# Attention block with two-level Strassen products: some VectorE work of the first image placed elsewhere, and inner sums of two outer factors taken in one instruction

## The chip, the cores and the metric

The kernel runs on one core of one Trainium2 chip. The metric is the device time of one execution in microseconds (us); lower is better. In the profile the engines are called PE (TensorE, matrix products), PEld (its weight loads), DVE (VectorE), ACT (ScalarE), POOL (GpSimd) and SP (SyncE, which issues DMAs).

## The reference

Sixteen images x of 512 channels by 32x32 places, all in fp32. Each is normalised over 8 groups of 64 channels, goes through attention with 4 heads of 128 channels over its 1024 places, is projected, and is added to x.

```python
xg = x.reshape(b, NUM_GROUPS, -1)
xn = ((xg - mu) * rsqrt(var + EPS)).reshape(b, c, h, w) * gamma + beta
q, k, v = split(einsum('oc,bchw->bohw', qkv_w, xn) + qkv_b, 3)   # to heads
attn = softmax(einsum('bhnd,bhmd->bhnm', q, k) * dh ** -0.5)
out = einsum('bhnm,bhmd->bhnd', attn, v)
return x + einsum('oc,bchw->bohw', proj_w, out) + proj_b
```

## The kernel before

**Products.** Scores and the weighted sum over values are plain fp32 products of 128 x 128 by 512 columns (`scores`, L964, tile `s`; `weighted_sum`, L1058, tile `po`). The three linear layers go by Winograd's form of Strassen's scheme, which takes seven products for eight, applied twice: seven outer factors, and in each seven inner products. The right-hand operand is called b. In one level, its four blocks b11, b12, b21, b22 give four sums: t1 = b12 - b11, t2 = b22 - t1, t3 = t2 - b11, t4 = b21 - t2; t2 needs t1, and t3 and t4 need t2. `FACTORS` says which operands each of the products 1 to 7 takes: product 1 b11, product 2 b21, product 3 b22, product 4 t4, product 5 t1, product 6 t2, product 7 t3.

**Outer level.** `halves` (L324) makes the outer blocks of an image out of four tiles of 128 x 1024 (x, the normalised input, or o, the output of the heads): each tile holds two blocks of 512 columns side by side. The outer t1 is written over b12, in the same tile; t2, t3 and t4 have tiles of 128 x 512 of their own, two of each (`KC` is 2). `sums_of_b` (L342) computes them on VectorE.

**Inner level.** `two_levels` runs the outer factors in four groups, `OUTER` = (1, 5), (2, 6), (7, 4), (3): a group holds one or two outer factors, whose inner products stand side by side in one PSUM bank of 512 columns, 256 columns for each factor. So group 0 works on the outer b11 and t1, group 2 on the outer t3 and t4. `make_sum` (L657) computes the inner sums of a group: one tile of 128 x 512 takes the sum for both outer factors, and a loop over i issues one VectorE subtraction of 128 x 256 for each. `mm` (L690) issues the products, ACT copies partial results out of PSUM (L565), VectorE adds them up (L715), adds groups together (L768) and adds the bias (`finish`, L827 for queries and keys, L943 and L946 for the projection). A group's products run in the order 1, 2, 6, 5, 7, 4, 3 (`ORDER`).

**Which sums are made where.** Each image has two query/key calls (`qk_groups`, pairs 0 and 1), one value call (`v_groups`) and one projection call (`proj_groups`). The calls of pair 0 make the inner sums and, from the second image on, keep them in DRAM, from where the value call loads them; pair 1 and the projection make their own. For pair 0 of the next image, the sums t1 and t2 of group 0 are taken with high priority behind the last running sum of the softmax denominators in the stage of head 1 (`added[b - 1, 1, NB - 1]`, L983).

**Order.** Each engine's instruction order is fixed before the run by a planner. It takes instructions in the order of their priorities, as they become ready by its own estimate of durations. The kernel steers it: `high_priority` moves an instruction ahead, `issue_after` puts one behind another on its engine, `keep_in_program_order` (called `pin` in the first image) holds the written order.

**First image.** `open_image` (L1328) writes the order out by hand. After the statistics of the upper two channel chunks, the value products of the first image start (`v_units`, one level, L845, with weights `wv`); the lower two chunks go through their group statistics, whose reciprocal root is taken by POOL (L89, `rstd`). Meanwhile VectorE computes sums of the value weights: s1 = a21 + a22, s2 = s1 - a11, s3 = a11 - a21 (written over a21), s4 = a12 - s2. Then `shift` yields, for each lower chunk, the shift (L1351), and the chunk's first half is normalised (L111 on VectorE for chunk 2, L108 on ACT for chunk 3), then the second halves. The outer t2 follows (L1342), then t3 (L1421), s3 of the value weights (L1422), t4 (L1424) and s4 (L1425), which are not pinned but stand behind t2.

Of the kernel before, what the change touches and what calls it, by code (L numbers as in the profile page):

```python
# [10 lines left out]
F32 = mybir.dt.float32  # L11
# [5 lines left out]
P = 128  # L17
# [4 lines left out]
HALF = 512  # L22
# [156 lines left out]
KC = 2  # L179
Q = 256  # L180

OUTER = ((1, 5), (2, 6), (7, 4), (3,))
# [3 lines left out]
def fast_path(ctx, tc, x, sources, out, consts, flag, dims):  # L186
# [6 lines left out]
    nc = tc.nc  # L193
    B, C, N, NCC, NH2, NB, GC, SCALE = dims
# [9 lines left out]
    tpool = ctx.enter_context(tc.tile_pool(name="t", bufs=1))  # L204
# [113 lines left out]
    def normalise(b, c, half, on_scalar=True):  # L318
        t = xs[b, c][:, ts(half, HALF)]
        sc, sh, i = scaled[b, c]  # L320
        return norm.apply(t, t, sc, sh, i, on_scalar)


    def halves(tiles, prefix):  # L324

        b = {
            f"b{r + 1}{h + 1}": [tiles[2 * r + k][:, ts(h, HALF)] for k in range(KC)]
            for r in range(2) for h in range(2)
        }
        b["t1"] = b["b12"]  # L330
        for n in ("t2", "t3", "t4"):
            b[n] = [
                tpool.tile([P, HALF], F32, tag=f"{prefix}{n}{k}", name=f"{prefix}{n}{k}")
                for k in range(KC)
            ]
        return b

    def sums_of_b(b, rows=(1, 2, 3), chunks=range(KC)):
# [149 lines left out]
    wv, beside, between = {}, {}, {}  # L488
# [58 lines left out]
    def run(units):  # L547
        for u in units:
            u()
# [54 lines left out]
    def two_levels(name, site, b, blocks, finish, sums="make", homes="BBBB", prepare=None):  # L604
# [7 lines left out]
        haves, pairs = [{} for _ in OUTER], {}  # L612
# [10 lines left out]
        def sum_tile(g, m):  # L623
            k = int(m[1]) - 1
            tag = f"in_{m}" if homes[g] == "B" else f"ot{2 + k // 2}{k % 2}"
            if homes[g] == "C":
                if k % 2 == 0:
                    pairs[g] = ppool.tile([P, N], F32, tag="p", name=f"{name}_{g}_{m}")
                t = pairs[g][:, ts(k % 2, HALF)]
            else:  # L630
                t = tpool.tile([P, HALF], F32, tag=tag, name=f"{name}_{g}_{m}")
            haves[g][m] = t.rearrange("p (i q) -> p i q", q=Q)
            return haves[g][m][:, : len(OUTER[g])]

        def inner_block(g, i, m):
            if m[0] == "t":
                return haves[g][m][:, i, :]
            outer = blocks()[FACTORS[OUTER[g][i]][1]]
            return outer[int(m[1]) - 1][:, ts(int(m[2]) - 1, Q)]

        def make_sum(g, m):
            n = len(OUTER[g])
            to = sum_tile(g, m)
            a, c = {
                "t1": ("b12", "b11"), "t2": ("b22", "t1"), "t3": ("t2", "b11"),
                "t4": ("b21", "t2"),
            }[m]
            with ExitStack() as order:
                if sums == "keep" and g == 0 and m in ("t1", "t2"):


                    order.enter_context(tc.issue_after(added[b - 1, 1, NB - 1].ins))
                    order.enter_context(tc.high_priority(URGENT))
                if (b, site) == (0, 1) and (g > 0 or m in ("t3", "t4")):
                    order.enter_context(tc.issue_after(beside["scores"].ins))
                for i in range(n):
                    nc.vector.tensor_sub(  # L657
                        to[:, i, :], inner_block(g, i, a), inner_block(g, i, c)
                    )
            if sums == "keep":  # L660
                t = dpool.tile([P, n, Q], F32, tag=f"{m}_{g}", bufs=1, name=f"kept_{m}_{g}")
                inner_kept[b, g, m] = t
                nc.gpsimd.dma_start(t, to)  # L663
# [292 lines left out]
    def where(s):  # L956
        bh, j = divmod(s, NB)
        return (*divmod(bh, HEADS), j)
# [362 lines left out]
    def warm(n, name):  # L1321

        acc = ps_s.tile([P, HALF], F32, tag="s", name=name)
        for _ in range(n):
            ins = nc.tensor.matmul(acc[:, :P], avg, avg, start=True, stop=True)  # L1325
            tc.keep_in_program_order(ins)

    def open_image(units):  # L1328


        pin = tc.keep_in_program_order
        mvs[0] = gn.tile([P, NCC, 2], F32, tag="mv", name="mv_0")
        upper, lower = slice(0, KC), slice(KC, NCC)

        def steps(these, *pinned):
            for i, step in enumerate(these):
                ins = step()
                if i in pinned:
                    pin(ins)

        def sum_(o, i, j, add=False):
            return pin((nc.vector.tensor_add if add else nc.vector.tensor_sub)(o, i, j))  # L1342

        def shift(r):

            mu, sc = norm.result
            sh = gn.tile([P, KC], F32, tag="sh", name="sh")
            for i, c in enumerate(range(r.start, r.stop)):
                o = slice(i, i + 1)
                scaled[0, c] = sc, sh, i  # L1350
                pin(nc.vector.scalar_tensor_tensor(  # L1351
                    sh[:, o], mu[:, o], sc[:, o], beta_sb[:, c : c + 1], ALU.mult, ALU.add
                ))
                yield c

        def stats_on_scalar(c):
            mean, var = mvs[0][:, c, 0:1], mvs[0][:, c, 1:2]
            junk = lpool.tile([P, N], F32, tag="tt", name="junk_0")
            off = gn.tile([P, 1], F32, tag="off", name="off")
            root = math.sqrt(N)  # L1360
            pin(nc.scalar.activation(
                junk, xs[0, c], AF.Identity, scale=1.0 / N, accum_out=mean
            ))
            pin(nc.scalar.mul(off, mean, -1.0 / root))
            pin(nc.scalar.activation(
                junk, xs[0, c], AF.Square, bias=off, scale=1.0 / root, accum_out=var
            ))

        warm(14, "warm_0")
        for c in range(KC):  # L1370
            steps(norm.chunk_steps(mvs[0], xs[0, c], c), 0, 1, 2)
        with tc.high_priority(URGENT):
            g = norm.group_steps(mvs[0][:, upper, :], 0, -1.0)
            steps(g[:1], 0)
            warm(2, "warm_1")
            steps(g[1:7], 0, 1, 2, 3, 4, 5)
            warm(9, "warm_2")

        stats_on_scalar(KC)
        pooled = g[7]()  # L1380
        pin(pooled)
        with tc.issue_after(pooled.ins):
            for t, src in ((qkb_sb, qk_b), (vb_sb, v_b), (projb_sb, proj_b)):
                nc.gpsimd.dma_start(t, src)
        steps(g[8:], 0)
        for c in shift(upper):
            pin(normalise(0, c, 0, False))
        for c in range(KC):
            pin(normalise(0, c, 1))
        steps(norm.chunk_steps(mvs[0], xs[0, NCC - 1], NCC - 1), 0, 1, 2)  # L1390
        xb[0] = halves([xs[0, c] for c in range(NCC)], "x")
        bl = xb[0]
        g = norm.group_steps(mvs[0][:, lower, :], KC, -1.0)

        def urgent(these, *pinned):
            with tc.high_priority(URGENT):
                steps(these, *pinned)

        between[1, 1, 0] = [lambda: urgent(g[:1], 0)]
        run(units[:2])  # L1400
        sum_(bl["t1"][0], bl["b12"][0], bl["b11"][0])
        sum_(wv["s1"], wv["a21"], wv["a22"], True)
        urgent(g[1:5], 0, 1, 2, 3)
        sum_(bl["t1"][1], bl["b12"][1], bl["b11"][1])
        between[0, 5, 0] = [lambda: urgent(g[5:6], 0)]
        run(units[2:3])
        urgent(g[6:7], 0)
        with tc.high_priority(URGENT):
            beside["pow"] = g[7]()
            pin(beside["pow"])  # L1410
        sum_(wv["s2"], wv["s1"], wv["a11"])
        urgent(g[8:], 0)
        for c in shift(lower):
            pin(normalise(0, c, 0, c % 2 == 1))
        for c in range(KC, NCC):
            pin(normalise(0, c, 1, c % 2 == 1))
        for k in range(KC):
            last = sum_(bl["t2"][k], bl["b22"][k], bl["t1"][k])
        with tc.issue_after(last.ins):
            for k in range(KC):  # L1420
                nc.vector.tensor_sub(bl["t3"][k], bl["t2"][k], bl["b11"][k])  # L1421
            nc.vector.tensor_sub(wv["s3"], wv["a11"], wv["a21"])  # L1422
            for k in range(KC):
                nc.vector.tensor_sub(bl["t4"][k], bl["b21"][k], bl["t2"][k])  # L1424
            nc.vector.tensor_sub(wv["s4"], wv["a12"], wv["s2"])  # L1425
        return last
# [19 lines left out]
    for s in range(steps + 1):  # L1446
        units = []
        if s < steps:
            b, h, j = where(s)
# [9 lines left out]
        for half in range(NH2):  # L1459
# [21 lines left out]
            n = (len(units) + 1) // 2  # L1481
# [150 lines left out]
```

## Time and profile before

| what | us |
|---|---|
| median of 3 runs | 3137.39 (3136.8 to 3137.7) |
| the profiled execution | 3137.81 |
| its span, first to last instruction | 3136.2 |
| PE busy (10412 matmul records, two for each fp32 product) | 3129.6 |
| VectorE busy (4683 instructions) | 2667.9 |
| ACT busy | 1447.4 |
| POOL busy | 512.2 |
| mean granted TensorE clock | 1.000 |

By stage (windows of the trace, us):

| stage | length | PE busy | DVE busy | ACT busy |
|---|---|---|---|---|
| value products of the first image, 11.14 to 35.7 | 24.56 | 24.56 | 23.09 | 7.26 |
| first query/key products, 35.7 to 62.2 | 26.50 | 26.25 | 26.19 | 9.62 |
| all images after that, 62.2 to 3111 | 3048.80 | 3048.80 | 2596.09 | 1422.00 |

How to read the profile: a row of a timeline gives start, duration, engine, line, operation, "out<-in" by the program's tile names with buffer numbers left out, the shape, and how many instructions of that kind were merged into the row; in square brackets stands the engine's idle time before it and what ended it. A row of the groups gives the busy time, the mean duration in ns of one, and the idle time before. Durations of instructions on one engine can overlap: the next VectorE instruction may start before the one before it ends. Ends of matmuls are modelled, so PE's real losses are read from the distances of starts. One image takes about 194.5 us; the same pattern returns at that distance.

### The profile page before, as it was taken

The numbers are of one execution on the slowest core, as the hardware profiler recorded it, in microseconds if no ns is written. First come the engines' busy times: TensorE is split into PE (matmuls) and PEld (weight loads), VectorE is DVE, ScalarE is ACT, GpSimd is POOL, SyncE is SP. The second block draws the span as 40 slices with busy tenths as digits, with TensorE's granted clock in tenths as the row PEclk, the third lists the DMA queues.
The fourth block names the chain that finished last, engine by engine and source line by source line (L and its number), as shares of the span: only waits on it lengthen the run. The fifth ranks groups of instructions, "written<-read, shape, count | busy, mean of one in ns | idle before, by whom it ended". The sixth has DMA issues, their size and how long they took to land.

```text
span 3136.2 us, 34085 instructions
## 1 busy us (share of the span) xinstructions
PE 3129.6 (100%) x10412; PEld 2200.4 (70%) x10412; DVE 2667.9 (85%) x4683; ACT 1447.4 (46%) x2655; POOL 512.2 (16%) x922
## 2 busy tenths in 40 slices
PE   9999999999999999999999999999999999999999
PEld 7567777777777777777777777777777777777765
DVE  8988889788897888978799787997879978799787
ACT  3545435354354543545435454454534535345433
POOL 0121121111211112111121101212012120121200
PEclk9999999999999999999999999999999999999999
DMA  5554554545555455554555545555455554555641
GB/s 176 170 192 149 197 172 165 165 153 189 175 167 165 147 194 172 166 168 145 197 170 167 170 144 191 169 176 168 145 185 172 176 175 140 179 169 178 193 128 45
DMA packets 210363, 522.59 MB, mean 167 GB/s; under 512 B 32368, under 2 KB 65776, under 8 KB 210176
## 3 DMA queue, kind: packets, MB, share of 16 engines
q1 hardware_dynamic: 132320, 278.26, 29.1%
q0 software_dynamic: 65184, 207.75, 19.6%
q10 hardware_dynamic: 12672, 34.35, 3.3%
q8 instruction: 86, 1.41, 0.2%
q14 instruction: 101, 0.83, 0.1%
HBM read 387.07 MB, written 133.17 MB: 166 GB/s over the span
## 4 chain that ended last, share of the span: by engine, by line
PE 100%; DVE 0%; issue 0%
PE po L1058 28%; PE s L964 28%; PE qk_x L690 12%; PE qk_y L690 9%; PE pp_x L690 6%; PE v_x L690 6%; PE pp_y L690 4%; PE v_y L690 4%; PE v_x L845 0%; PE warm L1325 0%; PE lx L1163 0%; PE v_y L845 0%; PE last_x L690 0%; PE v_z L845 0%; PE lv L1163 0%; PE lw L1163 0%
## 5 line engine op out<-in xcount | busy, mean ns | idle before, releaser
L964 PE MATMUL s<-qk,qk 128*128 128x512 f32 x2048 | 1045.8, 592 | 0.2 <-DVE qk L827 0.2
L1058 PE MATMUL po<-p,v 128*128 128x512 f32 x2048 | 1045.4, 592 | 0.0
L970 ACT ACTIVATE p<-s 128x512 f32<-128x512 f32 x1024 | 610.5, 596 | 877.6 <-PE s L964 853.3
L1058 PEld LDWEIGHTS po<-p,v 128*128 128x128 f32 x2048 | 616.2, 301 | 375.2 <-issue 258.5
L983 DVE TENSOR_TENSOR tot<-tot,p 128x1024 f32<-128x1024 f32 x385 | 470.0, 1221 | 133.6 <-ACT p L970 132.6
L964 PEld LDWEIGHTS s<-qk,qk 128*128 128x128 f32 x2048 | 389.0, 190 | 68.9 <-issue 12.9
L690 PEld LDWEIGHTS qk_x<-qk_t,w 128*128 128x128 f32 x1344 | 254.4, 190 | 153.3 <-issue 95.5
L690 PE MATMUL qk_x<-qk_t,w 128*128 128x256 f32 x1344 | 353.3, 379 | 0.0
L565 ACT COPY qk_u<-qk_x 128x512 f32<-128x512 f32 (+1 forms) x256 | 136.3, 532 | 238.0 <-PE qk_x L690 238.0
L896 POOL DMA_DIRECT2D vd<-vu x120 | 66.4, 553 | 957.3 <-DVE vu L888 955.1
L715 DVE TENSOR_TENSOR qk_r<-qk_y,qk_u 128x512 f32<-128x512 f32 (+1 forms) x256 | 158.2, 618 | 34.2 <-ACT qk_u L565 21.7
L947 POOL DMA_DIRECT2D out_y<-y x120 | 65.1, 543 | 643.4 <-DVE groups L300 401.3
L715 DVE TENSOR_TENSOR v_r<-v_y,v_u 128x512 f32<-128x512 f32 (+1 forms) x120 | 76.1, 634 | 107.6 <-ACT v_u L565 77.4
L690 PE MATMUL v_x<-v_t,w_v 128*128 128x256 f32 x630 | 165.3, 379 | 0.0
L690 PE MATMUL pp_x<-pp_t,w_proj 128*128 128x256 f32 x630 | 165.3, 379 | 0.0
L663 POOL DMA_DIRECT2D kept_t<-qk_t x240 | 129.6, 542 | 217.0 <-DVE qk_t L657 191.3
L690 PEld LDWEIGHTS pp_x<-pp_t,w_proj 128*128 128x128 f32 x630 | 119.7, 190 | 62.5 <-issue 35.9
L690 PEld LDWEIGHTS v_x<-v_t,w_v 128*128 128x128 f32 x630 | 119.7, 190 | 59.0 <-issue 34.4
L901 POOL DMA_DIRECT2D v<-vd x240 | 139.9, 590 | 68.7 <-issue 38.2
L690 PE MATMUL qk_y<-x,w 128*128 128x256 f32 x512 | 142.0, 379 | 0.0
L827 DVE SCALAR_TENSOR_TENSOR qk<-qk_r,qkb_sb,qk_r 128x512 f32<-128x512 f32 x192 | 137.7, 746 | 1.7
L888 DVE STREAM_TRANSPOSE vu<-vt 128x512 f32<-128x512 f32 x120 | 135.6, 1130 | 0.7 <-DMA vd<-vu 0.7
(251 smaller groups left out, 4417.6 us busy)
## 6 DMA issues: line engine op xcount, KB each, us to landing
w<-kept SPq DMA_DIRECT2D x90, 512.0 KB, 3.9
kept_t<-qk_t POOLq DMA_DIRECT2D x180, 256.0 KB, 2.8
v_t<-kept_t SPq DMA_DIRECT2D x180, 256.0 KB, 2.8
w<-kept SPq DMA_DIRECT2D x90, 384.0 KB, 3.4
rinv<-row ACTq DMA_DIRECT2D x63, 512.0 KB, 4.9
x<-in_x POOLq DMA_DIRECT2D x60, 512.0 KB, 4.8
vd<-vu POOLq DMA_DIRECT2D x120, 256.0 KB, 2.9
v<-vd POOLq DMA_DIRECT2D x240, 128.0 KB, 4.1
```

Source lines behind the costliest of these rows:

```text
L565: nc.scalar.copy(t[n][:, :width], t["x"][:, :width])
L663: nc.gpsimd.dma_start(t, to)
L690: latest["product"] = nc.tensor.matmul(acc[:, ts(i, Q)], have["w"][t][:, i, slot, :], inner(i, bn), start=(first and i == 0), stop=True, s ...
L715: latest["outer"] = nc.vector.tensor_add(dst, view(a), view(c))
L827: return nc.vector.scalar_tensor_tensor(st[b, h][:, ts(half, HALF)], a, qkb_sb[:, i : i + 1], c, ALU.add, ALU.add)
L888: nc.vector.transpose(u.rearrange("p (q i j) -> p j q i", q=n, i=BLK), t.rearrange("p (j q i) -> p j q i", q=n, i=BLK),)
L896: nc.gpsimd.dma_start(rows[which][ts(h, P), :], u)
L901: nc.gpsimd.dma_start(vs[b, pair][ts(q, BLK), half].rearrange("m h (k i) j -> m (h k) (i j)", k=n), rows[which].rearrange("(k m) (q e) -> ...
L964: latest["score"] = nc.tensor.matmul(sc, ks[b, h][:, ts(j, P)], qs[b, h][:, ts(half, HALF)], start=True, stop=True)
L970: exps[s] = nc.scalar.activation(ps[s][:, ts(half, HALF)], sc, AF.Exp, scale=SCALE)
L983: added[b, h, j] = nc.vector.tensor_add(tot[b, h][:, i], tot[b, h][:, i], ps[s][:, i])
L1058: summed = nc.tensor.matmul(po[half], v_block(b, h, j), ps[s][:, i], start=(j == 0), stop=(j == NB - 1),)
```

## The change

There are three edits.

1. `halves` puts the outer t3 and t4 of x side by side into one tile of 128 x 1024 (for o they stay apart), and keeps the two-block tiles under the keys 0 (b11 and t1, for x and o) and 2 (t3 and t4, for x). `make_sum` then takes, for groups 0 and 2 of the query/key calls and group 0 of the projection, both outer factors in one subtraction of 128 x 512 whose operands are two pieces of 256 columns each (`both_blocks`); the other groups keep the loop. The last image's projection, which has no such tiles, keeps the loop too.
2. In `open_image`, s3 of the value weights is computed directly behind s2, pinned, instead of between the outer t3 and t4.
3. In `open_image`, `list(shift(lower))` issues the shifts of both lower chunks first and then the normalisations, instead of shift, normalisation, shift, normalisation.

```diff
@@ halves @@
+        b[0] = tiles[:KC]
+        b["t2"] = tiles_of("t2")
+        if prefix == "x":
+            b[2] = tiles_of("t34", N)
+            b["t3"], b["t4"] = ([t[:, ts(i, HALF)] for t in b[2]] for i in range(2))
+        else:
+            b["t3"], b["t4"] = tiles_of("t3"), tiles_of("t4")
@@ two_levels @@
+        def both_blocks(g, m):
+            if m[0] == "t":
+                return haves[g][m][:, : len(OUTER[g]), :]
+            t = blocks()[g][int(m[1]) - 1].rearrange("p (i c q) -> p i c q", i=2, c=2)
+            return t[:, :, int(m[2]) - 1, :]
...
-                for i in range(n):
-                    nc.vector.tensor_sub(
-                        to[:, i, :], inner_block(g, i, a), inner_block(g, i, c)
-                    )
+                if g in blocks():
+                    nc.vector.tensor_sub(to, both_blocks(g, a), both_blocks(g, c))
+                else:
+                    for i in range(n):
+                        nc.vector.tensor_sub(
+                            to[:, i, :], inner_block(g, i, a), inner_block(g, i, c)
+                        )
@@ open_image @@
         sum_(wv["s2"], wv["s1"], wv["a11"])
+        sum_(wv["s3"], wv["a11"], wv["a21"])
         urgent(g[8:], 0)
-        for c in shift(lower):
+        for c in list(shift(lower)):
             pin(normalise(0, c, 0, c % 2 == 1))
...
         with tc.issue_after(last.ins):
             for k in range(KC):
                 nc.vector.tensor_sub(bl["t3"][k], bl["t2"][k], bl["b11"][k])
-            nc.vector.tensor_sub(wv["s3"], wv["a11"], wv["a21"])
             for k in range(KC):
                 nc.vector.tensor_sub(bl["t4"][k], bl["b21"][k], bl["t2"][k])
```

More of the change, by code (lines that the diff above doesn't have):

```diff
@@ L330, in halves, with tiles_of @@
         b["t1"] = b["b12"]
-        for n in ("t2", "t3", "t4"):
-            b[n] = [
-                tpool.tile([P, HALF], F32, tag=f"{prefix}{n}{k}", name=f"{prefix}{n}{k}")
+        def tiles_of(n, width=HALF):
+            return [
+                tpool.tile([P, width], F32, tag=f"{prefix}{n}{k}", name=f"{prefix}{n}{k}")
                 for k in range(KC)
             ]
+        b[0] = tiles[:KC]
[5 more added lines that the diff above has]
+            b["t3"], b["t4"] = tiles_of("t3"), tiles_of("t4")
         return b
```

## The prediction

> **What bounds the kernel.** I read the page first: busy shares (part 1), then the chain that ended last (part 4).
>
> ```profile
> PE 3129.6 (100%) x10412; PEld 2200.4 (70%) x10412; DVE 2667.9 (85%) x4683; ACT 1447.4 (46%) x2655; POOL 512.2 (16%) x922
> ...
> PE 100%; DVE 0%; issue 0%
> ```
>
> TensorE (PE) is the bound from end to end. Of the span of 3136.2 us, 6.6 are visibly idle on PE: 1.7 before its first matmul and about 4.5 behind its last, where no edit reaches. What PE loses besides is hidden in records that begin a little late, so I compared the starts of its matmuls with the usual spacing (0.430 us for 512 columns, 0.216 for 256). Beyond that spacing PE loses 4.4 us in all: 1.3 before 35 us, 1.7 between 35 and 62 us, 0.07 once in each of images 2 to 15 (0.94 together), 0.4 at the tail. All that this change can win lies in the second and third of these.
>
> Then the timeline of VectorE (DVE) in the first image, where two waits stand:
>
> ```profile
> 15.81 0.69 DVE L1342 TENSOR_TENSOR wv<-wv 128x512 f32<-128x512 f32 x1
> 17.12 0.16 DVE L76 TENSOR_TENSOR sc<-rstd,gamma_sb 128x2 f32<-128x2 f32 x1 [0.62 <-POOL rstd L89]
> ...
> 18.73 0.69 DVE L1342 TENSOR_TENSOR xt<-x,x 128x512 f32<-128x512 f32 x1
> 19.83 0.69 DVE L1342 TENSOR_TENSOR xt<-x,x 128x512 f32<-128x512 f32 x1 [0.40 <-ACT x L108]
> ```
>
> Last, the place in the steady images where an inner sum is closest to holding PE. I went through the spare time of every product behind the DVE row that feeds it; this one is the shortest of all sums, and it looks the same in images 2 to 15 (image 2 shown: DVE, weight loads, PE).
>
> ```profile
> 331.46 0.76 DVE L657 TENSOR_TENSOR qk_t<-x 128x256 f32<-128x256 f32 x2
> 332.14 0.76 DVE L657 TENSOR_TENSOR qk_t<-x,qk_t 128x256 f32<-128x256 f32 x2
> 332.67 0.79 PEld L690 LDWEIGHTS qk_x<-qk_t,w 128*128 128x128 f32 x4 [0.38 <-issue]
> 332.81 0.69 DVE L946 TENSOR_TENSOR y<-y,pp_r 128x512 f32<-128x512 f32 x1
> 332.84 1.03 PE L690 MATMUL qk_x<-qk_t,w 128*128 128x256 f32 x4
> 333.41 0.75 DVE L943 SCALAR_TENSOR_TENSOR y<-pp_r,projb_sb,y 128x512 f32<-128x512 f32 x1
> 333.70 1.03 PE L690 MATMUL qk_y<-qk_t,w 128*128 128x256 f32 x4
> ```
>
> The first row is t1 of outer factors 1 and 5, the second their t2; product 6 (qk_x at 332.84) reads t2, product 5 (qk_y at 333.70) reads t1. t2 of the first factor is done at 332.14 + 0.42 = 332.56.
>
> **The change, part by part.** *s3 moved.* One 128x512 subtraction (start to start 0.60) leaves its place at 21.64 and goes behind s2 into the 0.62 idle before 17.12: 15.81 + 0.60 = 16.41, next free 17.01. It fits, so it costs nothing; if rstd came sooner it would cost at most 0.60 on the normalisation. No other reader of the raw a21 is left by then (s1 read it at 13.71). It issues no DMA; SP's stores of wv_a can go some 4 us earlier, with the weight loads already issued before them. *Both shifts first.* The second shift moves from 18.03 to about 17.5, so ACT's normalise of chunk 3 starts about 0.45 before its 18.28, and the 0.40 wait at 19.83 goes. The first normalise on DVE is later by about 0.1; it was done at 18.12, and the weight load that needs it stands at 18.44.
>
> *Two sums in one.* Eight pairs fewer in each of 32 query/key calls (groups 0 and 2) and four in each of 15 projections (group 0): 256 + 60 = 316 pairs. A pair takes 0.67 (331.46 to 332.14 is 0.68), one 512-wide instruction 0.60 (332.81 to 333.41), so 0.07 each, 22 us of DVE time. The strided views cost nothing by the nearest rows:
>
> ```profile
> L657 DVE TENSOR_TENSOR qk_t<-x,qk_t 128x256 f32<-128x256 f32 x256 | 105.9, 433 | 2.2 <-PE qk_x L690 0.7
> L456 DVE TENSOR_TENSOR w<-w,w 128x256 f32<-128x256 f32 x6 | 2.6, 428 | 0.0
> ```
>
> L456 reads and writes two pieces of 128 apart from each other, L657 one piece. Almost all of the 22 us is off the path: DVE idles again between 289 and 306 us waiting for PE and ACT, so what is saved before that is waited away. In the first image DVE is hardly idle from 20.4 to 56 us and gains 0.60 + 0.40 + 8 x 0.07 = 1.6 us, but PE's 1.7 us lost there end mostly with ACT's copies of qk_x and with the chain last product, eviction, L827, first score. DVE ends 0.12 of it alone (at 44.87) and some 0.2 of the end chain: I take 0.3 gained, bounds 0 and 1.2 (all stalls that DVE ends). The 0.07 per image is an eviction at 327.09, behind DVE rows that are not merged and run without idle from 305: I take 0, bound 0.94.
>
> **What the merge takes away.** t2 reads what t1 writes. Now t1 of the second factor lies between, and hides the latency. Merged, t2 stands directly behind its own input. Rows for that:
>
> ```profile
> 315.07 0.42 DVE L657 TENSOR_TENSOR pp_t<-o 128x256 f32<-128x256 f32 x1
> 315.40 0.15 DVE L101 TENSOR_TENSOR sh<-beta_sb,t 128x4 f32<-128x4 f32 x1
> 315.48 0.74 DVE L943 SCALAR_TENSOR_TENSOR y<-pp_r,projb_sb,y 128x512 f32<-128x512 f32 x1
> 316.14 0.68 DVE L715 TENSOR_TENSOR pp_r<-pp_y,pp_u 128x512 f32<-128x512 f32 x1
> 316.74 0.41 DVE L657 TENSOR_TENSOR pp_t<-o,pp_t 128x256 f32<-128x256 f32 x1
> ...
> 320.68 0.68 DVE L715 TENSOR_TENSOR pp_r<-pp_y,pp_u 128x512 f32<-128x512 f32 x1
> 321.40 1.22 DVE L768 TENSOR_TENSOR pp_r<-pp_r,pp_r 128x1024 f32<-128x1024 f32 x1
> ```
>
> At 321.40 a dependent instruction starts 0.72 behind its input instead of 0.60. At 315.07 a single t1 and its t2 stand 1.67 apart: the planner, which fixes each engine's order beforehand, put three others between. And a late release costs PE this much: the eviction done at 327.09 held a product due at 327.18 (its pair takes 0.66 instead of 0.59), so the loss is release + 0.16 - due. Product 6 is due at 332.84, hence t2 has to be done by 332.68. The three ways:
>
> - A, t2 directly behind: 331.46 + 0.72 + 0.69 = 332.87, loss 0.19 an image, 14 images: 2.7 us.
> - B, one 512-wide between (L946 is ready): 331.46 + 0.60 + 0.60 + 0.69 = 333.35, loss 0.67, 14 times 9.4; image 1 (due 138.30, t1 at 136.31) about 0.1 more: 9.5 us.
> - C, as B on DVE, but PE's order changes too: product 5 needs only t1 (done by 332.15) and lasts 0.86; with it first, product 6 is due at 333.70, past 333.35 + 0.16, loss 0.
>
> Behind the waiting t2 stand L946 and L943 of the projection's outputs, which go to DMA; no product waits for them. The other merged sums have over 1 us to spare (t3 of the same group, next, 1.07).
>
> The Trainium skill, "VectorE: DVE Perf Modes", section "The DRAIN you can't avoid", says that a next op waits for the pipe whether chained or not, and that a semaphore between two costs nothing extra. By that, t2 would follow 0.60 behind t1 and A would cost 0.07 x 14 = 1.0 us instead of 2.7; the row's 0.72 differs from it, and I go by the row. The same page's section "Rules for kernel authors" asks for fewer ops and not fewer semaphores, and speaks for the merge; it says nothing of a dependent one.
>
> **Which way.** I take C as likeliest. The planner picks by readiness: in the first image's second call PE took qk_y<-qk_t at 64.79 before qk_x<-qk_t at 66.51, against the written order. With t2 0.8 us later than now, product 5 should be taken first. Sum: 3137.81 of the profiled run (span 3136.2 and 1.6 around it) - 0.3 = 3137.5; the median shown lies 0.4 lower, at 3137.39, so **3137.1**.
>
> **Rivals.** B is the slower one. It decides when t2 is done past 332.68 while the planner still thinks it ready for product 6. For it: the planner is off by some tenths here already, since it had PE wait at 327.18 in 14 images, and an eviction (L715 at 329.40) is taken 1.5 us after the product it reads (at 327.18, 0.66 long) is done. Against it: it needs an error of at least some 0.5 us in this direction. Time: 3137.4 - 0.3 + 9.5 = 3146.6. A: 3137.4 - 0.3 + 2.7 = 3139.8; against it that the planner fills such gaps whenever something is ready. A further rival is that all DVE-ended stalls go (1.2 + 0.9): 3135.3; even that is 0.07%, so nothing here can be faster by over 0.2% (6.3 us), about what a measurement of this kernel can tell from no change. Last, that other orders change with so many durations and PE is held in new places, bounded only by B's size: 0.05.
>
> **Chances.** C 0.44, A 0.15, full gain 0.05, B 0.31, other slower 0.05. Same = 0.44 + 0.15 + 0.05 less 0.01 for an unseen gain = 0.63; slower 0.36; faster 0.01. The likeliest's own range is 3136.0 to 3138.0; it leaves out more than 2 in 10, so the range reaches to B and its error: 3135.8 to 3147.5.
>
> **What would show it.** DVE: 4683 - 316 = 4367 instructions on the page, L657's successors 512 wide at about 690 ns, no 0.62 and 0.40 waits before 20 us. PE at about 332.8: qk_y<-qk_t before qk_x<-qk_t (C), the old order with the weight load 0.25 late (A) or 0.7 late (B), "PEld qk_x <- DVE qk_t" new in the waits. Wrong if PE loses time at other products, or if the 35 to 62 us stretch gets longer.

## The result, and the profile after

The changed kernel takes 3148.67 us (median of 7 runs, 3148.44 to 3149.54); the kernel before, run beside it on the same chip, 3137.35 (7 runs, 3136.8 to 3137.7). The ratio is 1.0036, 95% interval 1.0027 to 1.0046: 11.3 us slower. In the profiled executions the span grew from 3136.2 to 3147.2, by 11.0 us (the profiled execution of the kernel before, 3137.81, lies 0.5 above its median), and the rest of this section looks for those 11.0. Images are counted from 0.

The page of the changed kernel: busy shares (part 1), the chain that ended last (part 4), and from the groups the row of the linear layers' products.

```profile
PE 3133.0 (100%) x10412; PEld 2199.2 (70%) x10412; DVE 2650.6 (84%) x4367; ACT 1447.9 (46%) x2655; POOL 511.9 (16%) x922
...
PE 85%; DVE 12%; issue 2%; ACT 0%; DMA 0%; DVEq 0%; POOL 0%
...
L710 PE MATMUL qk_x<-qk_t,w 128*128 128x256 f32 x1344 | 354.6, 380 | 7.5 <-DVE qk_t L674 7.5
```

VectorE has 316 instructions fewer and 17.3 us less busy time, and the kernel is slower. The chain, PE alone before, now runs over VectorE for 12% of the span; that isn't time lost, only the way back from the places where a product waited for a sum. The last row names them: 7.5 us of visible idle time ahead of products that read `qk_t`, ended by `make_sum` (now L674). The waits of PE count them (engine, tile and line, what it waited for: us in total, times, the longest):

```profile
PE qk_x L710 <- DVE qk_t L674: 7.5, 15, 0.5
PE warm L1345 <- DVE avg L247: 1.7, 1, 1.7
PE pm L82 <- DVE mv L52: 0.5, 1, 0.5
PE s L984 <- DVE qk L847: 0.2, 1, 0.2
```

Fifteen times: once in each image from the second on. The timeline of image 2 at the place that the prediction showed:

```profile
332.21 0.68 DVE L674 TENSOR_TENSOR qk_t<-x 128x512 f32<-128x512 f32 x1
...
332.71 1.02 PE L1078 MATMUL po<-p,v 128*128 128x512 f32 x2
332.81 0.68 DVE L966 TENSOR_TENSOR y<-y,pp_r 128x512 f32<-128x512 f32 x1
333.41 0.68 DVE L674 TENSOR_TENSOR qk_t<-x,qk_t 128x512 f32<-128x512 f32 x1
334.01 0.74 DVE L963 SCALAR_TENSOR_TENSOR y<-pp_r,projb_sb,y 128x512 f32<-128x512 f32 x1
334.20 0.73 PEld L710 LDWEIGHTS qk_x<-qk_t,w 128*128 128x128 f32 x4 [1.18 <-ACT p L990]
334.24 1.10 PE L710 MATMUL qk_x<-qk_t,w 128*128 128x256 f32 x4 [0.50 <-DVE qk_t L674]
...
335.17 1.03 PE L710 MATMUL qk_y<-qk_t,w 128*128 128x256 f32 x4
```

t1 of both outer factors, one projection row (L966), t2 of both. The two records of `po` keep PE until 332.71 + 2 x 0.43 = 333.57; there product 6 was due. t2 is done at 333.41 + 0.68 = 334.09, the weight load begins at 334.20 and the product at 334.24: 0.67 us lost (0.50 of it shows as idle, because the ends of matmuls are modelled). Its four records take 1.10 instead of 1.03, another 0.07. PE keeps the old order, product 6 (qk_x<-qk_t) before product 5 (qk_y<-qk_t). In images 2 to 15 the loss is 0.74 each time; in image 1, where a 128x1024 transpose (L1012, 1.23 us) stands between t1 and t2, it is 0.66. 14 x 0.74 + 0.66 = **11.0 us**, as much as the spans differ. Smaller terms beside it cancel: the first value product starts 0.12 later, the trace ends 0.34 sooner behind its last product, and in image 6 a `qk_y` product loses 0.24, the only new loss of PE at another product. Its weight load waits there for a VectorE row, 15 us after VectorE itself has waited 0.80 for a DMA:

```profile
1223.14 0.73 PEld L710 LDWEIGHTS qk_y<-x,w 128*128 128x128 f32 x4 [0.38 <-DVE qk_r L735]
1223.15 1.13 PE L710 MATMUL qk_y<-x,w 128*128 128x256 f32 x4
```

The same pair, a DMA wait of 0.8 to 0.9 us and then a loss at `qk_y`, stands in experiments 7 and 8 and in no other kernel here (experiment 4 has a DMA wait of 0.41 at that place and no loss); whether the change brings the DMA wait about wasn't tried.

The first image, VectorE, where the two waits stood:

```profile
15.93 0.69 DVE L1362 TENSOR_TENSOR wv<-wv 128x512 f32<-128x512 f32 x1
16.54 0.68 DVE L1362 TENSOR_TENSOR wv_a<-wv,wv_a 128x512 f32<-128x512 f32 x1
17.24 0.16 DVE L76 TENSOR_TENSOR sc<-rstd,gamma_sb 128x2 f32<-128x2 f32 x1
...
18.73 1.33 DVE L1362 TENSOR_TENSOR xt<-x,x 128x512 f32<-128x512 f32 x2
```

Both waits are gone: s3 fills the first (16.54), and the two `xt` rows now stand back to back. VectorE's work in the stage of the first query/key products (35.7 to 62.2 us before, 35.8 to 62.3 now) fell from 26.19 to 24.75 us. PE's loss there, by the starts of its matmuls, went only from 1.69 to 1.65: the 0.12 at 44.87 went, and 0.08 came at 46.12.

### The profile page after: what moved, and what is told of

It is laid out like the page before. It is cut to its first block, busy times and chain, and to the rows that moved or that the text cites. A ratio compares the mean times of both kernels' runs of the same rounds, so it can differ in the third digit from the quotient of the medians.

```text
span 3147.2 us, 33761 instructions
## 1 busy us (share of the span) xinstructions
PE 3133.0 (100%) x10412; PEld 2199.2 (70%) x10412; DVE 2650.6 (84%) x4367; ACT 1447.9 (46%) x2655; POOL 511.9 (16%) x922
## 4 chain that ended last, share of the span: by engine, by line
PE 85%; DVE 12%; issue 2%; ACT 0%; DMA 0%; DVEq 0%; POOL 0%
PE s L984 24%; PE po L1078 23%; PE qk_x L710 12%; PE qk_y L710 9%; PE v_x L710 6%; PE v_y L710 4%; PE pp_x L710 3%; DVE tot L1003 2%; PE pp_y L710 2%; DVE y L966 2%; DVE pp_r L735 1%; DVE y L963 1%; DVE pp_r L788 1%; DVE pp_t L677 1%; DVE qk_t L674 1%
## 5 line engine op out<-in xcount | busy, mean ns | idle before, releaser
L1003 DVE TENSOR_TENSOR tot<-tot,p 128x1024 f32<-128x1024 f32 x385 | 469.4, 1219 | 129.1 <-ACT p L990 128.9
```

What stands on the lines that cost most here:

```text
L1003: added[b, h, j] = nc.vector.tensor_add(tot[b, h][:, i], tot[b, h][:, i], ps[s][:, i])
```

## The experiments

Eight kernels were run. Theory: the whole loss is product 6 of group 0 in the kept calls, held because t2 ends later, and nothing else in the change matters to the time.

**1. The first image's edits alone** (the kernel before with edits 2 and 3).

```diff
+        sum_(wv["s3"], wv["a11"], wv["a21"])
...
-        for c in shift(lower):
+        for c in list(shift(lower)):
...
-            nc.vector.tensor_sub(wv["s3"], wv["a11"], wv["a21"])
```

> The kernel before with the two edits of the first image alone (s3 behind s2, both shifts first), no merged sums. Theory (all of the loss sits at product 6 of group 0 in the calls that keep their sums, and comes from the merged t1 and t2): within 0.3 us of the kernel before, so 3137.0 to 3137.5; PE's 1.7 us lost between 35 and 62 us shrink by 0.1 at most. Rival (the moved work of the first image holds PE later): 3138 or more, with new losses before 62 us.

Measured: 3137.19 us against 3137.23, ratio 1.0000 (0.9990 to 1.0009). PE loses 1.65 us between 35 and 62 us, as in the changed kernel. The edits of the first image neither cost nor bring anything that can be measured.

**2. The changed kernel, with the kept t1 and t2 of group 0 in their loop again.**

```diff
+                early = sums == "keep" and g == 0 and m in ("t1", "t2")
-                if g in blocks():
+                if g in blocks() and not early:
```

> The changed kernel, but t1 and t2 of group 0 in the 15 calls that keep their sums go back to the loop of two 256-wide subtractions; all other sums stay merged, the first image's edits stay. Theory: product 6 is due again with its sum done 0.1 us before, no wait of PE for qk_t; 3137.0 to 3137.6. Rival (merged sums cost something elsewhere too, or the wide strided subtraction is slow): 3139 or more.

Measured: 3137.48 against 3137.23, ratio 1.0001 (0.9991 to 1.0010), span 3135.8; no product waits for `qk_t`. The other 286 merged sums cost nothing that can be measured.

**3. Those 30 sums merged and nothing else** (the kernel before, with both blocks in one subtraction where `sums == "keep" and g == 0 and m in ("t1", "t2")`).

> The kernel before, with t1 and t2 of group 0 in the 15 calls that keep their sums merged, and nothing else changed: 30 pairs instead of 316. Theory: the whole loss is here: 14 x 0.74 + 0.67 = 11.0 us, so 3148.0 to 3148.8, with PE's wait for qk_t at 15 places. Rival (the loss is spread over all merges): 30/316 of 11 us, so about 3138.5.

Measured: 3148.29 against 3137.23, ratio 1.0035 (1.0022 to 1.0047), span 3146.6: 0.74 us at product 6 in each of 14 images and 0.66 in image 1. So 30 of the 316 merges hold the whole loss, and the rival that spreads it falls.

**4. The changed kernel with product 5 ahead of product 6** in group 0 of the kept calls: the order that the prediction had expected of the planner, written out.

```diff
-            return [
+            units = [
...
+            if sums == "keep" and g == 0:
+                units[2], units[3] = units[3], units[2]
+            return units
```

> The changed kernel with product 5 written ahead of product 6 in group 0 of the calls that keep their sums; every merge stays. Theory: product 5 needs t1 alone and takes 0.86 us, so product 6 is due 0.86 later and t2, done 0.74 too late before, is in time with 0.1 to spare: no wait, 3136.8 to 3137.5. Rival (the late t2 also holds product 7 or ACT's copy of product 6, which now comes 0.86 later): a new wait at product 7 or 4 and 3139 or more.

Measured: 3137.79 against 3137.23, ratio 1.0001 (0.9992 to 1.0011), span 3136.4. The median is 0.3 above the expected band; PE's losses in the trace are those of the kernel before, so the 0.3 has no place that I could name. The timeline of this kernel at the same place:

```profile
331.50 0.68 DVE L674 TENSOR_TENSOR qk_t<-x 128x512 f32<-128x512 f32 x1
332.11 0.68 DVE L969 TENSOR_TENSOR y<-y,pp_r 128x512 f32<-128x512 f32 x1
...
332.71 0.68 DVE L674 TENSOR_TENSOR qk_t<-x,qk_t 128x512 f32<-128x512 f32 x1
332.87 1.03 PE L710 MATMUL qk_y<-qk_t,w 128*128 128x256 f32 x4
...
333.74 1.03 PE L710 MATMUL qk_x<-qk_t,w 128*128 128x256 f32 x4
```

VectorE's order is unchanged, t2 is as late behind t1 as in the changed kernel (331.50 to 333.39), and product 6 at 333.74 starts exactly 0.87 behind product 5. The lateness costs nothing once another ready product stands before it.

**5 and 6. One of the two merged alone** (the kernel before, with one subtraction for t1 only, then for t2 only).

```diff
+                early = sums == "keep" and g == 0 and m == "t1"
+                if early:
+                    nc.vector.tensor_sub(to, both_blocks(g, a), both_blocks(g, c))
+                else:
+                    for i in range(n):
...
```

> The kernel before, with t1 alone in one instruction in the kept calls' group 0; t2 stays two of 256. Theory (the loss is the row put between t1 and t2, plus the half-width by which a wide t2 gives its first half later): t2's first half ends 0.60 + 0.60 + 0.42 = 1.62 us behind t1's start instead of the 1.88 of the changed kernel, so product 6 is held 0.74 - 0.26 = 0.48 us in each of images 2 to 15 and some 0.40 in image 1: 14 x 0.48 + 0.4 = 7.1, about 3144.4 us. Rival 1 (only the wide t2 is at fault: its first half comes with its last): no hold, about 3137.3. Rival 2 (it is the row between alone, whatever the widths): 0.60 an image less the 0.11 spare = 0.49 and the same in the next run.

> The kernel before, with t2 alone in one instruction in the kept calls' group 0; t1 stays two of 256. Theory: t2 reads what the second t1 has just written, so a row goes between all the same, and t2 ends 0.67 + 0.60 + 0.68 = 1.95 us behind the start of the first t1: held 0.74 + 0.07 = 0.81 in each of images 2 to 15 and some 0.73 in image 1, 14 x 0.81 + 0.73 = 12.1, about 3149.4 us, worse than both merged. Rival 1 (only the wide t2's later first half, no row between): 0.26 - 0.11 + 0.06 = 0.2 an image, 3 us, about 3140. Rival 2 (the row between alone): 0.49 an image, about 3144.4.

Measured: t1 alone 3144.06 against 3137.38, ratio 1.0021 (1.0012 to 1.0031); t2 alone 3149.30, ratio 1.0038 (1.0024 to 1.0052). Timeline of t1 alone, then of t2 alone:

```profile
331.88 0.68 DVE L666 TENSOR_TENSOR qk_t<-x 128x512 f32<-128x512 f32 x1
332.49 0.68 DVE L958 TENSOR_TENSOR y<-y,pp_r 128x512 f32<-128x512 f32 x1
...
333.09 0.75 DVE L669 TENSOR_TENSOR qk_t<-x,qk_t 128x256 f32<-128x256 f32 x2
...
333.65 1.10 PE L702 MATMUL qk_x<-qk_t,w 128*128 128x256 f32 x4 [0.23 <-DVE qk_t L669]
```

```profile
332.42 0.75 DVE L669 TENSOR_TENSOR qk_t<-x 128x256 f32<-128x256 f32 x2
333.09 0.68 DVE L958 TENSOR_TENSOR y<-y,pp_r 128x512 f32<-128x512 f32 x1
...
333.69 0.68 DVE L666 TENSOR_TENSOR qk_t<-x,qk_t 128x512 f32<-128x512 f32 x1
...
334.52 1.10 PE L702 MATMUL qk_x<-qk_t,w 128*128 128x256 f32 x4 [0.57 <-DVE qk_t L666]
```

In both a row of the projection stands between t1 and t2, although only one of them is wide. The product is held 0.47 us an image in the first (0.40 at its start, 0.07 inside) and 0.81 in the second; 0.48 and 0.81 were expected. The first starts 0.14 behind the end of t2's first half (333.09 + 0.42 = 333.51), so a wide t2 costs by itself the 0.26 by which its first half comes later. Rival 1, without the row between, falls in both runs: it had no hold in the first and 0.2 us an image in the second. Rival 2, the row alone, had 0.49 for both runs; the first can't tell it from the theory's 0.48, and the second, with 0.81, rules it out.

**7. The changed kernel with t1 and t2 let in one row sum earlier.**

```diff
-                    order.enter_context(tc.issue_after(added[b - 1, 1, NB - 1].ins))
+                    order.enter_context(tc.issue_after(added[b - 1, 1, NB - 2].ins))
```

> The changed kernel with one number changed: the kept calls' t1 and t2 may start after the previous image's row sum before last instead of after the last one. Theory (product 6 is held only because t2 comes 0.74 us after its due time): t1 and t2 then stand before the last row sum on VectorE, with the projection's add still between them; t2 ends about 1.2 us sooner, past its due by nothing, product 6 isn't held, and the row sum behind them (1.2 us later) has only the next score's buffer to give free: 3136.8 to 3137.8 us, span 3136.0 to 3136.8. Rival (VectorE is short of time at this place, so what is moved ahead only moves the hold on to another row, as the row sum, the evictions of qk or the softmax's p): some 0.3 to 1 us an image again, 3141 to 3151.

Measured: 3137.40 against 3137.38, ratio 1.0000 (0.9991 to 1.0010), span 3136.1.

```profile
329.90 0.68 DVE L674 TENSOR_TENSOR qk_t<-x 128x512 f32<-128x512 f32 x1
...
330.50 0.68 DVE L966 TENSOR_TENSOR y<-y,pp_r 128x512 f32<-128x512 f32 x1
...
331.10 0.68 DVE L674 TENSOR_TENSOR qk_t<-x,qk_t 128x512 f32<-128x512 f32 x1
...
331.70 1.22 DVE L1003 TENSOR_TENSOR tot<-tot,p 128x1024 f32<-128x1024 f32 x1
...
333.00 1.03 PE L710 MATMUL qk_x<-qk_t,w 128*128 128x256 f32 x4
```

t1, L966 and t2 stand in the same order, but before the last row sum (L1003) instead of behind it. t2 is done at 331.78, 1.2 us ahead of the product, and no product waits for the row sum that is now later (PE's one new loss is 0.29 us in image 6, behind a DMA wait as in the changed kernel). VectorE has room at this place: with the trigger one row sum earlier, neither the row between nor the wide t2 costs time.

**8. t2 computed twice**, to see whether the planner ever takes product 5 first.

```diff
-                    nc.vector.tensor_sub(to, both_blocks(g, a), both_blocks(g, c))
+                    for _ in range(2 if sums == "keep" and (g, m) == (0, "t2") else 1): nc.vector.tensor_sub(to, both_blocks(g, a), both_blocks(g, c))
```

> The changed kernel with t2 of the kept calls' group 0 computed twice, one subtraction behind the other: 15 instructions more, t2 done later still. In the order that the planner then writes out, PE takes product 5 (qk_y<-qk_t) and a score product ahead of product 6 in images 2 to 15, while in image 1 one half of product 5 goes ahead. Theory (the forecast's idea was sound, but t2 was too little late for the planner to act on it; what costs time is only where product 6 stands): t2 is done 2 x 0.60 + 0.06 us later, about 3.15 behind t1's start, and product 6 is due 1.72 later than in the changed kernel, so it is held 0.27 instead of 0.74 in each of 14 images; in image 1 t2 comes 1.13 + 0.68 later and product 6 is due 0.43 later, held some 2.0. 14 x 0.27 + 2.0 = 5.8: about 3143.2 us, so faster than the changed kernel by 5 though it does more. Rival (the place of product 6 does not matter, the late sum holds PE all the same through what it feeds): the hold grows by the second subtraction to 0.74 + 1.26 = 2.0 an image, 3137.4 + 28 + 2 = 3167.

Measured: 3144.73 against 3137.31, ratio 1.0023 (1.0013 to 1.0033): 3.9 us faster than the changed kernel, with 15 instructions more.

```profile
333.58 0.68 DVE L674 TENSOR_TENSOR qk_t<-x 128x512 f32<-128x512 f32 x1
...
334.95 1.03 PE L710 MATMUL qk_y<-qk_t,w 128*128 128x256 f32 x4
...
335.81 1.02 PE L984 MATMUL s<-qk,qk 128*128 128x512 f32 x2
336.05 0.68 DVE L674 TENSOR_TENSOR qk_t<-x,qk_t 128x512 f32<-128x512 f32 x1
...
336.88 1.10 PE L710 MATMUL qk_x<-qk_t,w 128*128 128x256 f32 x4
...
338.69 1.09 PE L710 MATMUL qk_x<-qk_t,w 128*128 128x256 f32 x4
```

Product 5 (334.95) and a score product (335.81) now go ahead. Product 6 loses 0.28 us in each of 14 images (0.27 expected) and 1.94 in image 1 (2.0 expected). What I had left out are 0.07 an image at product 7 (338.69), behind ACT's copy of product 6's bank, and waits of some 0.4 and 0.3 in images 6 and 10 at qk_y: 14 x (0.28 + 0.07) + 1.94 + 0.7 = 7.5 of the 7.9 us by which the span is longer than before. The planner does act on readiness; it takes product 5 first when t2 is one subtraction later still.

None of these kernels beats the kernel before: experiments 1, 2, 4 and 7 stand within 0.02% of it, and the intervals reach to about 0.1%.

## Why the prediction went wrong, point by point

**The bound and the place: right.** PE was the bound, the change could win at most 2.1 us, and the one sum without time to spare was t2 of group 0 in the kept calls. Experiment 3 shows that these 30 of 316 merged pairs make the whole loss, experiment 2 that the others make none that can be measured.

**VectorE's side: right.** The waits of 0.62 and 0.40 went, 4367 instructions were left, a row went between t1 and t2 as in B and C, and in images 2 to 15 it was the projection's row that was named (now L966). The 0.07 for each pair came out as 17.3 / 316 = 0.055 of busy time. None of it was worth time. The Trainium skill, "VectorE: DVE Perf Modes", section "Rules for kernel authors", asks for fewer ops. Here 316 fewer gave nothing that can be measured, and 30 of them cost 11 us.

**The step that failed: C taken before B.** The prediction said "With t2 0.8 us later than now, product 5 should be taken first", from one place in the first image where PE took qk_y ahead of qk_x. It wasn't: PE's order stayed, and t2 was late for it. The fact behind C was sound: with product 5 first the loss is nil (experiment 4). The idea that the planner goes by readiness was sound too (experiment 8). What was wrong is how late t2 must come before the planner acts. It left PE's order as it was with t2 0.74 us too late, and with 0.81 in experiment 6; B was said to need "an error of at least some 0.5 us in this direction", and the two rows cited for B (the stall of 0.07 in 14 images, the eviction taken 1.5 us late) spoke for such an error at just this stage. The place cited for C is in the first image, with 1.72 us between the two products. No run shows the planner's own estimates, so it stays open whether it took t2 for ready or kept to the written order for another reason; experiments 6 and 8 put the turning point between a t2 that ends 0.07 later than in the changed kernel (PE's order unchanged) and one that ends 1.3 later.

**The size of B: 9.5 forecast, 11.0 found.** Two terms were too small. (a) From t2's end to the product I took 0.16, from an eviction's row. Here it is 0.15 to the start and 0.07 inside the product, 0.22 in all: 14 x 0.06 to 0.07 = 0.9. (b) In image 1 I put the same 128x512 filler between; the planner put the transpose of the row sums there (1.23 us), so 0.66 instead of 0.1: 0.6. Together 1.5. The time found lies 2.1 above B's 3146.6: these 1.5, the 0.3 of gain that B's sum had taken off, and 0.3 by which the medians differ more than the profiled spans. The upper end of the range was B and 0.9 more, and all three lay on the same side, so it stopped 1.2 us short.

**The gain of the first image: 0.3 forecast, 0.04 found** in the trace, and none by the clock (experiment 1). One stall that VectorE ended went, another one came 1.2 us later: what VectorE gained there was nearly all waited away at the next place.

**The rest.** A (t2 directly behind t1) didn't happen in group 0. Its 0.72 is borne out by group 2 of the changed kernel, where a merged t2 stands directly behind its t1 in 15 calls and starts 0.73 behind it (rows in the last section); the prediction was right to go by its row and not by 0.60. Of its signs of being wrong, one showed in a small way: PE lost 0.24 us at another product, in image 6. The stall of 0.07 behind the eviction stayed, as said. B was the rival on the other side, with its place and mechanism right.

## What to carry to other kernels

Two pairs t1a, t1b, t2a, t2b merged into t1, t2 save an instruction each but lose the cover that t1b gave t2a; here the planner filled the gap in the calls that keep their sums with a whole foreign row (in group 2 it left t2 directly behind t1), and the first half of t2 comes later too. So before merging, take the spare time of the consumer of the second sum and hold it against filler + half a width (here 0.60 + 0.26 against 0.11), and leave the loop, move the trigger, or put another ready product first where it doesn't fit. And when a forecast hangs on what a planner will do, go by what it does at that very stage, not by one place where it did what is hoped for.

## What the runs showed of the hardware

A product that starts late because a sum was late loses more than the lateness: in the changed kernel and in experiments 3, 5, 6 and 8 the weight load begins 0.11 to 0.12 us behind the sum's end (0.05 behind the eviction in the kernel before), the product 0.03 to 0.04 later, and its four records take 1.10 instead of 1.03 us. Why the two kinds of wait differ by 0.06 wasn't tried.

In the changed kernel a 128x512 sum that reads the sum directly ahead of it starts 0.73 us behind it, and the next row, which reads neither, 0.61 behind that. These are t1 and t2 of group 2 and a row of the outer sums of o (the first of 15 places where this t2 stands directly behind its t1; all show 0.73):

```profile
251.11 0.69 DVE L674 TENSOR_TENSOR qk_t<-xt 128x512 f32<-128x512 f32 x1 [0.73 <-PE qk_y L710]
251.84 0.69 DVE L674 TENSOR_TENSOR qk_t<-xt,qk_t 128x512 f32<-128x512 f32 x1
252.45 0.69 DVE L352 TENSOR_TENSOR ot<-o,o 128x512 f32<-128x512 f32 x1
```
